# Phase A of a two-layer adaLN kernel: rows modulated on GpSimd instead of transposed back on TensorE

## The chip, the cores and the metric

The kernel runs on one core of a Trainium2 chip. A core has TensorE (PE) for matmuls, VectorE (DVE), ScalarE (ACT) and GpSimd (POOL) for the rest, and SyncE (SP), which issues most of the DMAs. The metric is the device time of one execution in microseconds; the median of some timed runs is given. A profile is one execution more, taken with the hardware profiler.

## What is computed

Two transformer layers act on x, of shape (4, 1024, 256), fp32 throughout. A row of x is a token; a batch is one of the four sequences. Each layer normalises x, scales and shifts it per batch (the modulation), runs an attention-like block, adds the result times a gate, and does the same again with a mixture of experts. Phase A is the first half of layer 0 and the modulation and routing of its second half. Cut to that:

```python
mod = (silu(L0_c) @ L0_wmod).reshape(4, 6, 1, -1)
sa, ca, ga, sb, cb, gb = (mod[:, i] for i in range(6))
ga, gb = (the sign of each) * maximum(abs(each), 0.25)
h = layernorm(x) * (1 + ca) + sa
x = x + ga * attn(h)            # bilinear attention, no softmax
h = layernorm(x) * (1 + cb) + sb
x = x + gb * experts(h)         # 8 experts, the best 2 of each token
```

The attention has no softmax, so for a batch it reduces to h times a 256 x 256 matrix (block-diagonal in the kernel's layout), made from h's Gram matrix, the queries, the combiners and the gate ga.

## The kernel before, in words

Phase A loads x, computes shifts, scales and gates, and then does for each batch a first half (`first_half`) and a second half (`second_half`). A batch has 8 chunks of 128 tokens, worked on in two groups (g = 0, 1) of four.

A group's rows are normalised by ACT (`normalised`, L968, four instructions of 128x256, into a buffer xn1 or xn2). PE transposes them to features on partitions (`to_features`, L1008, eight transposes). ACT takes them out of PSUM and modulates in the same instruction (L1013), since shift and scale are one number per partition there; this gives h1T or h2T. But the rows with tokens on partitions are needed too, modulated. So `to_tokens` transposes h1T or h2T back (L1035, eight transposes, named pm_b) and ACT copies the result out (L1040, two copies of 128x512) into h1 or h2.

In the first half the modulated rows h1 feed the Gram matrix (`gram`, L1102, 32 matmuls a batch, after all of the batch's rows are there). Its diagonal blocks are multiplied with the combiners (`head_t1`, L1134) and the queries (`head_m`, L1155) and then with the gate ga0 (`head_m_out`, L1167); the result is md. In the second half h1T times md gives the attention's output (L1195), DVE adds it to x (L1205), and the new rows are normalised, transposed and modulated again. h2T feeds the router's logits (L1235), DVE picks the experts (`route`), and the modulated rows h2 are stored to DRAM, to `h_rows` (L1270), from which the expert phase gathers its tokens.

Shifts and scales are made with features on partitions (`mods_by_feature`, L883 on PE, then DVE into modT). The gates ga and gb are made as rows of four partitions (`gate_row`, `gate_of`), and `gates` spreads each batch's rows over 128 partitions with matmuls against a selecting matrix `pick` (`spread`, L335, named pm_bc); ACT copies them into ga0 and gb0 (L927, L928).

The order on PE, ACT, DVE and POOL is not the program's but that of a planner (`Plan`): each piece of work has an engine, a supposed duration, pieces that it comes after, buffers that it holds and a rank (low first). The planner plays the pieces through in time, and their instructions are written in the order in which they begin. `FIRSTS` and `SECONDS` are the ranks of the batches' halves. SP's DMAs are pieces too, but SP is not among the engines whose order is fixed (`ORDERED`), in Phase A. Buffers are counted in `Plan(...)`: three of xn1, two of xn2, one h1, four h2.

Ahead of the plan SP loads x (L218), small tensors, and the first contents of the two expert weight buffers (L236, L237; 1028 KB and 1152 KB, twice). They hold the last expert, so that blocks of that expert need no gather; they are first read by the expert phase. ACT's queue loads the modulation weights of layer 0 (L204); those of layer 1 come later into the same buffer, from SP, and are multiplied near the end of Phase A (L1319). Phase A ends with a chain that makes the lists of the experts' blocks (turn, total, close, limits, L440 to L761), after which POOL fetches the first rows of `h_rows` (L348) and PE starts on the experts (L1610).

Of the kernel before, what the change touches and what calls it, by code (L numbers as in the profile page):

```python
# [8 lines left out]
F32 = mybir.dt.float32  # L9
F16 = mybir.dt.float16  # L10
I32 = mybir.dt.int32
AF = mybir.ActivationFunctionType
ALU = mybir.AluOpType
# [124 lines left out]
def adaln_d2_kernel(  # L138
# [92 lines left out]


    w1buf = [pw.tile([P, W1ROW], F32, name=f"w1_{i}") for i in range(2)]
    w2buf = [pw.tile([P, W2ROW], F32, name=f"w2_{i}") for i in range(2)]
    for i in range(2):
        nc.sync.dma_start(w1buf[i], W1[(E - 1) * P :, :])  # L236
        nc.sync.dma_start(w2buf[i], W2[(E - 1) * P :, :])  # L237

    xgbuf = [pw.tile([P, D], F32, name=f"xg_{i}") for i in range(4)]
# [7 lines left out]
    for e in range(E):  # L247
        nc.gpsimd.memset(rank[:, e : e + 1], float(E - e))

    pick = pa.tile([B, B, P], F32, name="pick", bufs=1)  # L250
    nc.gpsimd.memset(pick, 0.0)
    nc.gpsimd.affine_select(
        out=pick,
        in_=pick,
        compare_op=ALU.not_equal,
        fill=1.0,
        base=0,
        pattern=[[-1, B], [0, P]],
        channel_multiplier=1,
    )  # L260
    ones16 = const.tile([P, P], F16, name="ones16")
# [46 lines left out]
    def silu_of(layer, cT):  # L308
        sT = small.tile([P, KD, B], F32, name=f"sT{layer}")
        nc.scalar.activation(sT, cT, AF.Silu)  # L310
        return sT

    def mod_rows(sT, w, at, n):

        pr = psum(ps_2, [B, n], "pm_mod")
        for k in range(KD):
            nc.tensor.matmul(
                pr, lhsT=sT[:, k, :], rhs=w[:, k, at : at + n], start=(k == 0), stop=(k == KD - 1)
            )
        return pr  # L320

    def gate_of(dst, src, scratch):
# [7 lines left out]
        nc.vector.scalar_tensor_tensor(dst, sign, -1.0, size, ALU.add, ALU.mult)  # L330

    def spread(b, rows):

        pb = psum(ps_m, [P, rows.shape[1]], "pm_bc")
        nc.tensor.matmul(pb, lhsT=pick[:, b, :], rhs=rows, start=True, stop=True)  # L335
        return pb

# [500 lines left out]

    modT = const.tile([P, 4, KD, B], F32, name="modT")
    SA, CA, SB, CB = range(4)  # L840
# [16 lines left out]

    plan = Plan(p1=3, p2=2, pm=3, xn1=3, h1T=2, h1=1, xn2=2, h2T=2, h2=4, t1=1)
    PE, ACT, DVE, POOL = "PE", "ACT", "DVE", "POOL"
# [14 lines left out]
    def mods_by_feature(which, column, at):  # L874
        ps = plan.slot("p1")

        def mm():
            pf = tiles["modT", which] = psum(ps_1, [P, 2 * KD, B], "pm_modT")
            for i in range(2):
                for q in range(KD):  # L880
                    c = column[i] * D + q * P
                    for k in range(KD):
                        nc.tensor.matmul(  # L883
                            pf[:, i * KD + q, :],
                            lhsT=wm0[:, k, c : c + P],
                            rhs=sT0[:, k, :],
                            start=(k == 0),
                            stop=(k == KD - 1),
                        )

        def out_():
            pf = tiles["modT", which]
            nc.vector.tensor_copy(modT[:, which[0], :, :], pf[:, :KD, :])
            nc.vector.tensor_scalar(
                modT[:, which[1], :, :], pf[:, KD:, :], 1.0, None, ALU.add
            )

        i = plan(PE, 1.8, mm, holds=[ps], at=at, rank=-1)
        return plan(DVE, 0.4, out_, after=[i], holds=[ps], rank=-1)

    def gate_row(i, column, at):
# [13 lines left out]
        )  # L915

    def gates(after):
        done = []
        for b in range(B):
            ps = plan.slot("pm")  # L920

            def mm(b=b):
                tiles["spread", b] = spread(b, gate_rows.rearrange("b i d -> b (i d)"))

            def out_(b=b):
                pb = tiles["spread", b]
                nc.scalar.copy(ga0[:, b, :], pb[:, :D])  # L927
                nc.scalar.copy(gb0[:, b, :], pb[:, D:])  # L928

            m = plan(PE, 0.9, mm, after=after, holds=[ps], rank=b - 0.4)  # L930
            done.append(plan(ACT, 0.8, out_, after=[m], holds=[ps], rank=b - 0.4))
        return done

# [65 lines left out]
    def to_features(b, g, key, slot, dst, held, shift, scale, after, rank):  # L999

        done = []
        for k in range(KD):
            ps = plan.slot("pm")

            def mm(k=k):
                pt = tiles["pt", key, k] = psum(ps_m, [P, 4, P], "pm_t")
                for i in range(4):
                    nc.tensor.transpose(  # L1008
                        pt[:, i, :], tiles["xn", key][:, i, k * P : (k + 1) * P], ident
                    )  # L1010

            def out_(k=k):
                nc.scalar.activation(  # L1013
                    dst()[:, k, :, :],
                    tiles["pt", key, k],
                    AF.Identity,
                    bias=modT[:, shift, k, b : b + 1],
                    scale=modT[:, scale, k, b : b + 1],
                )

            m = plan(PE, 0.55, mm, after=after, holds=[ps, slot, held], rank=rank)
            done.append(plan(ACT, 0.67, out_, after=[m], holds=[ps, held], rank=rank))
        return done

    def to_tokens(key, src, held, dst, to, after, rank):

        done = []
        for i in range(2):
# [10 lines left out]
            def out_(i=i):  # L1039
                nc.scalar.copy(dst()[:, 2 * i : 2 * i + 2, :], tiles["pb", key, i])  # L1040

            m = plan(PE, 0.55, mm, after=after, holds=[ps, held, to], rank=rank)
            done.append(plan(ACT, 0.6, out_, after=[m], holds=[ps, to], rank=rank))
        return done
# [12 lines left out]

    FIRSTS, SECONDS, SPLIT = [0.0, 1.89, 1.82, 2.75], [1.66, 2.89, 3.45, 2.92], 2

    def first_half(b, arrival):  # L1060

        rank = FIRSTS[b]
        held, to = plan.slot("h1T"), plan.slot("h1")
        hT = buffer(("h1T", b), "h1T", [P, KD, NC, P])
        h = buffer(("h1", b), "h1", [P, NC, D])
        whole = []
        for g in range(2):
            key, slot = (1, b, g), plan.slot("xn1")
            n = normalised(
                b, range(4 * g, 4 * g + 4), key, slot, lambda c: [], rank, arrival[g]  # L1070
            )
            cs = slice(4 * g, 4 * g + 4)
            f = to_features(
                b,
# [9 lines left out]
            )  # L1084
            whole += to_tokens(
                key,
                lambda cs=cs: hT()[:, :, cs, :],
                held,
                lambda cs=cs: h()[:, cs, :],
                to,  # L1090
                f,
                rank,
            )

        ps, gd, md = plan.slot("p1"), gds[b % 2], mds[b % 2]

        def gram(j, cs):
            if j == 0 and cs[0] == 0:
                tiles["gram", b] = psum(ps_1, [P, KD, P], "pm_gram")
            for c in cs:  # L1100
                hj = h()[:, c, j * P : (j + 1) * P]
                nc.tensor.matmul(  # L1102
# [12 lines left out]
        for j in range(KD):  # L1115
            for cs in (range(4), range(4, NC)):
# [5 lines left out]
                        after=m,  # L1122
                        holds=[ps, to],
                        rank=rank,
# [38 lines left out]
        def head_m_out():  # L1163
# [12 lines left out]
            head_m_out,  # L1176
            after=[m, gates0[b], *before],
            holds=[ps],
# [4 lines left out]
    def second_half(b):  # L1183
# [34 lines left out]
        for g in range(2):  # L1218
# [4 lines left out]
            hT2, held2 = buffer(("h2T", b, g), "h2T", [P, KD, 4, P]), plan.slot("h2T")  # L1223
            f = to_features(b, g, key, slot, hT2, held2, SB, CB, [*n, mods_b], rank)
            if b == SPLIT and g:
# [18 lines left out]
            if b == SPLIT:  # L1244
                of_batch["routed"] = ready[g][0]
            h2, to = buffer(("h2", b, g), "h2", [P, 4, D]), plan.slot("h2")
            backs[g] = (to_tokens(key, hT2, held2, h2, to, f, rank + 0.1), to, h2)
        for gs in routed:
# [16 lines left out]
            for g in gs:  # L1265
                back, to, h2 = backs[g]

                def store(g=g, h2=h2):
                    at = 4 * g * B * P
# [3 lines left out]
                        )[b],  # L1273
                        h2(),
                    )

                plan("SP", 4.0, store, after=back, holds=[to], rank=rank)

# [3 lines left out]

    mods_a = mods_by_feature((SA, CA), (0, 1), 7.5)
    mods_b = mods_by_feature((SB, CB), (3, 4), 12.0)
    rows_done = [gate_row(0, 2, 10.0), gate_row(1, 5, 12.0)]
    gates0 = gates(rows_done)
    for b in range(B):
# [21 lines left out]

    loaded = plan("SP", 0.3, load_wm1, after=[mods_a, mods_b, *rows_done])  # L1310
    for piece in range(3):
        ps = plan.slot("p2")
        m = loaded
        for k in range(KD):

            def mm(piece=piece, k=k):
                if k == 0:
                    tiles["rows1", piece] = psum(ps_2, [B, 2 * D], "pm_mod")
                nc.tensor.matmul(  # L1319
                    tiles["rows1", piece],  # L1320
                    lhsT=sT1[:, k, :],
                    rhs=tiles["wm1"][:, k, 2 * D * piece : 2 * D * (piece + 1)],
# [1133 lines left out]
```

## Time and profile before

| what | value |
|---|---|
| timed runs, median of 3 | 1171.77 us (1170.53 to 1175.14) |
| the profiled execution's own time | 1148.51 us |
| its span | 1146.5 us |
| mean granted TensorE clock | 0.988 |
| busy: PE, DVE, ACT, POOL | 1101.7, 589.4, 428.2, 413.8 us |
| first expert matmul (L1610) starts at | 124.98 us |
| last row store to h_rows issued at | 110.9 us |
| way back to rows, L1035 and L1040 | 128 transposes, 32 copies |
| spreading, L335, L927 and L928 | 8 matmul passes, 8 copies |

In a row of the profile, "out<-in" are the names of what is written and read, then come the shapes, "xN" is the number of instructions, then busy time and mean duration, and after the second bar the idle time ahead of them with what ended it. PEld is the weight load of PE, which overlaps its matmuls. A time in brackets in the timeline is the idle time just ahead of a line.

### The profile page before, as it was taken

To read this page: it belongs to the slowest core of one execution; us is meant where nothing else is said; L and a number is where in the kernel's file an instruction comes from. 1 tells how busy PE (TensorE), PEld (TensorE's weight loads), DVE (VectorE), ACT (ScalarE), POOL (GpSimd) and SP (SyncE) were. 2 spreads that over 40 slices of the span, in tenths; PEclk is the share of its full clock that TensorE was granted. 3 is DMA by queue.
4 is the path that set the end of the run, shared out by engine and by line. 5 is a ranking of instruction groups with operands and counts; after the bars stand their busy time and mean duration, and the time that the engine had idled before them with its cause. 6 is when DMAs were issued, how large, how long until landed. Compare 5 with 4: busy or idle time off the path is not lost. (4 is left out here: it accounts for less than half of the span.)

```text
span 1146.5 us, 18577 instructions
## 1 busy us (share of the span) xinstructions
PE 1101.7 (96%) x6244; PEld 873.2 (76%) x6244; DVE 589.4 (51%) x2243; ACT 428.2 (37%) x1156; POOL 413.8 (36%) x479
## 2 busy tenths in 40 slices
PE   9999899999999999999998999999999999999894
PEld 5997799999999999999988565665666676646651
DVE  7686332322122222222237598877677535787567
ACT  5967233323333322333325333423325325333321
POOL 2000334433443343334355452420125232536535
PEclk8999999999999999999999999999999999999988
DMA  9303423656441514242162221200028564337944
GB/s 341 121 23 111 140 83 102 218 170 202 133 153 37 190 38 152 74 152 80 38 216 71 74 65 47 65 19 19 0 78 245 167 169 137 102 99 214 283 131 142
DMA packets 88388, 140.50 MB, mean 123 GB/s; under 512 B 24730, under 2 KB 63136, under 8 KB 83684
## 3 DMA queue, kind: packets, MB, share of 16 engines
q0 software_dynamic: 31680, 69.61, 20.0%
q1 hardware_dynamic: 55508, 68.10, 18.5%
q10 hardware_dynamic: 1104, 1.58, 0.4%
q8 instruction: 51, 0.84, 0.3%
q14 instruction: 45, 0.37, 0.1%
HBM read 222.48 MB, written 30.57 MB: 221 GB/s over the span
## 5 line engine op out<-in xcount | busy, mean ns | idle before, releaser
L1622 ACT ACTIVATE hid<-p_h,w 128x128 f32<-128x128 f32 x544 | 154.9, 368 | 324.6 <-issue 263.7
L1610 PEld LDWEIGHTS p_h<-xT,w 128*128 128x128 f32 x2176 | 252.9, 192 | 7.8 <-DVE xT L1595 3.9
L1610 PE MATMUL p_h<-xT,w 128*128 128x128 f32 x2176 | 254.5, 275 | 4.0 <-DVE xT L1595 4.0
L1633 PE MATMUL p_y<-w,hid 128*128 128x256 f32 x1088 | 248.9, 382 | 0.0
L1890 PE MATMUL p_u<-hT,a 128*128 128x512 f32 x512 | 230.3, 596 | 2.4 <-ACT hf L1902 1.5
L348 POOL DMA_INDIRECT w<-in_W,g_wrow x134 | 133.8, 999 | 263.9 <-ACT hid L1622 121.4
L1633 PEld LDWEIGHTS p_y<-w,hid 128*128 128x128 f32 x1088 | 201.6, 190 | 24.6
L1890 PEld LDWEIGHTS p_u<-hT,a 128*128 128x128 f32 x512 | 93.8, 190 | 101.3 <-issue 89.9
L1595 DVE COPY xT<-pm_x 128x256 f32<-128x256 f32 x68 | 28.8, 424 | 177.0 <-PE pm_x L1590 176.8
L1644 DVE TENSOR_TENSOR y<-p_y,w 128x256 f32<-128x256 f32 x68 | 28.8, 424 | 172.1 <-PE p_y L1633 172.1
L1938 PE MATMUL p_f<-a,hf 128*128 128x256 f32 x512 | 115.3, 380 | 0.0
L348 POOL DMA_INDIRECT xg<-h_rows,g_row x68 | 65.7, 966 | 129.6 <-DVE g_hits L752 109.1
L1938 PEld LDWEIGHTS p_f<-a,hf 128*128 128x128 f32 x512 | 96.3, 190 | 15.5 <-issue 2.9
L348 POOL DMA_INDIRECT yg<-y,g_slot x64 | 61.5, 961 | 83.6 <-DVE x_sb L1467 45.2
L2203 PE MATMUL p_e<-we,xT 128*128 128x256 f32 x280 | 73.2, 393 | 4.1 <-DMA we<-in_ew 3.5
L1902 ACT ACTIVATE hf<-p_u,decay 128x512 f32<-128x512 f32 x56 | 38.1, 683 | 67.6 <-PE p_u L1890 65.1
L2203 PEld LDWEIGHTS p_e<-we,xT 128*128 128x128 f32 x280 | 50.1, 194 | 14.7 <-issue 5.5
L1986 POOL TENSOR_TENSOR x_sb<-x_sb,step 128x256 f32<-128x256 f32 x32 | 24.2, 758 | 99.3 <-DVE step L1979 87.5
L348 POOL DMA_INDIRECT xg<-ga_rows,ga_row x39 | 37.1, 950 | 53.2 <-DVE g_hits L752 19.4
L1530 DVE TENSOR_TENSOR h<-h,mod 128x256 f32<-128x256 f32 x128 | 50.9, 422 | 5.8 <-ACT h L1520 3.4
L1906 DVE SCALAR_TENSOR_TENSOR hf<-p_u,decay,hf 128x512 f32<-128x512 f32 x56 | 41.9, 748 | 17.2 <-PE p_u L1890 13.5
L2213 ACT COPY y<-p_e 128x256 f32<-128x256 f32 x70 | 25.8, 371 | 60.1 <-PE p_e L2203 27.2
(368 smaller groups left out, 1295.7 us busy)
## 6 DMA issues: line engine op xcount, KB each, us to landing
we<-in_ew SPq DMA_DIRECT2D x70, 256.0 KB, 3.8
y<-y SPq DMA_DIRECT2D x68, 128.0 KB, 1.8
ga_y<-y SPq DMA_DIRECT2D x39, 128.0 KB, 3.3
x_sb<-in_x SPq DMA_DIRECT2D x8, 512.0 KB
h_rows<-h SPq DMA_DIRECT2D x8, 512.0 KB, 3.6
gb_y<-y SPq DMA_DIRECT2D x31, 128.0 KB, 4.7
out_x<-x_sb SPq DMA_DIRECT2D x7, 512.0 KB, 3.1
a<-in_fw SPq DMA_DIRECT2D x6, 512.0 KB
```

The source lines that it names most:

```text
L348: return nc.gpsimd.indirect_dma_start(out=dst, out_offset=None, in_=table, in_offset=bass.IndirectOffsetOnAxis(ap=index, axis=0), bounds_c ...
L1530: nc.vector.tensor_tensor(h, h, mods1[(sc, sh)[i]][:, b, :], (ALU.mult, ALU.add)[i])
L1595: nc.vector.tensor_copy(xT, pt)
L1610: nc.tensor.matmul(p1[:, i, :], lhsT=w1[:, k * H + m * P : k * H + (m + 1) * P], rhs=xT[:, k, :], start=(k == 0), stop=(k == KD - 1),)
L1622: nc.scalar.activation(hid[:, m, :], p1[:, i, :], AF.Relu, bias=w1buf[j % 2][:, KD * H + m : KD * H + m + 1],)
L1633: nc.tensor.matmul(p2, lhsT=hid[:, m, :], rhs=w2[:, m * D : (m + 1) * D], start=(m == 0), stop=(m == KH - 1),)
L1644: nc.vector.tensor_tensor(y, p2, w2buf[j % 2][:, KH * D :], ALU.add)
L1890: nc.tensor.matmul(pu, lhsT=a[:, k, m * P : (m + 1) * P], rhs=made["n1", c, "hT"][:, k, :, :], start=(k == 0), stop=(k == KD - 1),)
L1902: nc.scalar.activation(made[key, m], made[key, m, 0], AF.Silu, scale=decays[c])
L1906: nc.vector.scalar_tensor_tensor(h, made[key, m, 1], decays[c], h, ALU.mult, ALU.mult)
L1938: nc.tensor.matmul(made[key, "p2", b], lhsT=made[key, m][:, b * P : (b + 1) * P], rhs=a1[:, m, :], start=(m == 0), stop=(m == KH - 1),)
L2203: nc.tensor.matmul(made[key, "p2"], lhsT=made[key, "xT"][:, k, :], rhs=made[key, "we"][:, k * D : (k + 1) * D], start=(k == 0), stop=(k == ...
```

## The change

Half of the groups no longer get their rows by the way back. For batch 1 in the first half, and for the groups (batch, g) = (0,0), (0,1), (1,0), (1,1), (2,0), (3,0) in the second, POOL modulates the normalised rows in place, with two multiplications and two additions of 128 x (2 x 256) each per group (`modulated`). It starts when PE has read the rows for their transposes. The other groups keep the transposes, and these now write over the normalised rows; h1 and h2 are gone, and xn1 and xn2 have four buffers each.

POOL needs shifts and scales as rows on all partitions (`spread0`). So modT, now ordered batch before feature half, is transposed by PE (one transpose for each pair), copied out by ACT, stored to DRAM by SP, and loaded back by SP with a partition broadcast (1 MB a pair). The gates go the same way: gate_rows to DRAM, then one broadcast load each into ga0 and gb0. `pick`, `spread` and `gates` go. The first loads of the expert weights move into the plan, after the broadcast loads, and layer 1's modulation weights come after them. The silu of c is padded with zeros from 4 to 64 columns for the matmuls of `mods_by_feature`. The ranks of the halves are others.

The diff, cut to its core:

```diff
-    for i in range(2):
-        nc.sync.dma_start(w1buf[i], W1[(E - 1) * P :, :])
-        nc.sync.dma_start(w2buf[i], W2[(E - 1) * P :, :])
...
-        sT = small.tile([P, KD, B], F32, name=f"sT{layer}")
-        nc.scalar.activation(sT, cT, AF.Silu)
+        sT = pa.tile([P, KD, ROUTER], F32, name=f"sT{layer}", bufs=1)
+        nc.vector.memset(sT, 0.0)
+        nc.scalar.activation(sT[:, :, :B], cT, AF.Silu)
...
-    plan = Plan(p1=3, p2=2, pm=3, xn1=3, h1T=2, h1=1, xn2=2, h2T=2, h2=4, t1=1)
+    plan = Plan(p1=3, p2=2, pm=3, xn1=4, h1T=2, xn2=4, h2T=2, t1=1)
...
+        def turn():
+            pr = tiles["rows0_ps", which] = psum(ps_m, [2 * B * KD, P], "pm_rows")
+            nc.tensor.transpose(
+                pr, modT[:, pair, :, :].rearrange("p w b k -> p (w b k)"), ident
+            )
...
+        def store():
+            nc.sync.dma_start(
+                mod_rows0[pair, :, :].rearrange("w b (k p) -> (w b k) p", p=P),
+                tiles["rows0", which],
+            )
+
+        def load():
+            nc.sync.dma_start(spread0[:, pair, :, :], mod_rows0[pair, :, :].partition_broadcast(P))
+
+        m = plan(PE, 0.12, turn, after=[d], holds=[ps], rank=-0.9)
+        a = plan(ACT, 0.25, turned, after=[m], holds=[ps], rank=-0.9)
+        q = plan("SP", 0.1, store, after=[a], rank=-0.9, lag=2.2)
+        return d, plan("SP", 0.1, load, after=[q], rank=-0.9, lag=4.5)
...
+    def modulated(b, key, slot, shift, scale, after, rank):
+
+        done = []
+        for i in range(2):
+            last = after
+            for of, op in ((scale, ALU.mult), (shift, ALU.add)):
+
+                def do(i=i, of=of, op=op):
+                    h = tiles["xn", key][:, 2 * i : 2 * i + 2, :]
+                    nc.gpsimd.tensor_tensor(
+                        h, h, spread0[:, of, b, :].unsqueeze(1).to_broadcast([P, 2, D]), op
+                    )
+
+                last = [plan(POOL, 1.45, do, after=last, holds=[slot], rank=rank)]
+            done += last
+        return done
...
-    FIRSTS, SECONDS, SPLIT = [0.0, 1.89, 1.82, 2.75], [1.66, 2.89, 3.45, 2.92], 2
+    FIRSTS, SECONDS, SPLIT = [0.0, 1.66, 1.65, 3.35], [1.8, 3.42, 3.5, 2.62], 2
+
+
+    POOL1, POOL2 = (1,), ((0, 0), (0, 1), (1, 0), (1, 1), (2, 0), (3, 0))
...
+            if b in POOL1:
+                whole += modulated(b, key, slot, SA, CA, [*turned, spread_a], rank)
+            else:
+                whole += to_tokens(key, slot, lambda cs=cs: hT()[:, :, cs, :], held, f, rank)
...
-            after=[m, gates0[b], *before],
+            after=[m, gate_loaded, *before],
...
-    gates0 = gates(rows_done)
+
+    def gates_out():
+        nc.sync.dma_start(gates0, gate_rows)
+
+    def gate_in(i, dst):
+        nc.sync.dma_start(dst, gates0[:, i, :].partition_broadcast(P))
+
+    q = plan("SP", 0.1, gates_out, after=rows_done, rank=-0.8, lag=2.2)
+    gate_loaded = plan("SP", 0.1, lambda: gate_in(0, ga0), after=[q], rank=-0.8, lag=3.5)
+
+    def first_weights():
+
+        for i in range(2):
+            nc.sync.dma_start(w1buf[i], W1[(E - 1) * P :, :])
+            nc.sync.dma_start(w2buf[i], W2[(E - 1) * P :, :])
+        gate_in(1, gb0)
+
+    weights0 = plan("SP", 0.5, first_weights, after=[spread_a, spread_b, gate_loaded])
...
-    loaded = plan("SP", 0.3, load_wm1, after=[mods_a, mods_b, *rows_done])
+    loaded = plan("SP", 0.3, load_wm1, after=[weights0])
```

## Prediction

> **What bounds the kernel now.** I first read the busy shares in 40 slices. TensorE (PE) is at 9 tenths nearly everywhere, while the granted clock and the DMA share show that the first slices are different: the queues are full and PE is not. The change touches only Phase A, which ends where the first expert matmul starts, so I cut that stretch out with the table of stages.
>
> ```profile
> core 0: us, PE busy (x) PEld busy (x) DVE busy (x) ACT busy (x) POOL busy (x), PEclk, DMA share, GB/s
> ...
> 23.00:26.00 3.00, 2.90 (x8) 1.43 (x9) 2.66 (x15) 1.36 (x5) 0.00 (x0) 0.56 1.03 422
> 26.00:29.00 3.00, 3.00 (x16) 3.00 (x16) 1.89 (x10) 2.71 (x7) 0.00 (x0) 0.50 1.00 416
> ...
> 32.00:109.00 77.00, 73.86 (x651) 68.40 (x650) 55.51 (x225) 60.48 (x118) 0.00 (x0) 1.00 0.21 71
> ```
>
> From 32 to 109 us PE runs 73.9 of 77 us, at full clock, with the DMA engines mostly idle and GpSimd (POOL) not used at all. ScalarE (ACT) is second with 60.5 us. So this stretch is a PE stream with some ACT waits. Before 32 us it is a chain of hand-offs behind the loads, at half clock for part of it. Next the groups of instructions of that stretch, PE's and then ACT's:
>
> ```profile
> L1035 PE MATMUL pm_b<-ident,h2T 128*128 128x128 f32 x56 | 8.2, 277 | 1.1 <-ACT h2T L1013 1.1
> L1035 PE MATMUL pm_b<-ident,h1T 128*128 128x128 f32 x48 | 7.1, 277 | 0.0
> ```
>
> ```profile
> L1040 ACT COPY h<-pm_b 128x512 f32<-128x512 f32 x26 | 14.1, 592 | 1.9 <-PE pm_b L1035 1.9
> ```
>
> These are the transposes back to rows, 8 pairs of weight load and matmul to a group of four chunks, and the two copies of 592 ns that follow. A matmul's 277 ns overlaps the next one, so its price is the spacing of starts, which the timeline gives. The timeline also has the start, the gate and the end:
>
> ```profile
> 23.10 1.83 PE L335 MATMUL pm_bc<-gate_rows,pick 4*128 4x512 f32 x2 [0.43 <-ACT h1T L1013]
> ```
>
> ```profile
> 36.08 0.59 DVE L1167 TENSOR_TENSOR md<-pm_m,ga 64x128 f32<-64x128 f32 x2
> ...
> 36.82 3.19 PE L1195 MATMUL pm_o<-md,h1T 128*128 128x128 f32 x24 [0.35 <-DVE md L1167]
> ```
>
> ```profile
> 88.16 0.92 PEld L1035 LDWEIGHTS pm_b<-ident,h2T 128*128 128x128 f32 x8
> ...
> 89.05 1.86 PEld L1235 LDWEIGHTS pm_l<-wr_sb,h2T 128*128 128x128 f32 x16
> ```
>
> ```profile
> 120.80 1.12 POOL L348 DMA_INDIRECT xg<-h_rows,g_row  x1 [109.15 <-DVE g_hits L752]
> ...
> 124.98 3.81 PE L1610 MATMUL p_h<-xT,w 128*128 128x128 f32 x32 [0.56 <-DVE xT L1595]
> ```
>
> Eight weight loads of the way back start at 88.16 and the next kind at 89.05: 0.89 us for 8, so 111 ns a pair. The last router matmul ends at 109.1; from there routing, list and first fetch are one serial chain to 120.8, and the experts start at 125.0. From there on PE is busy to the end. So I take it that a microsecond taken out before 109 moves everything after it by a microsecond.
>
> **What the Trainium skill says.** "TensorE: Matmul & The Clock Gate", LDWEIGHTS: the load time is the number of columns over 1.2, 107 ns for 128. The 111 ns agree: the stream is paced by weight loads. "GPSIMD Engine Reference", 3.1: a two-input fp32 add of 2048 elements takes 4497 ns. The trace has it smaller, and in another stage:
>
> ```profile
> L1986 POOL TENSOR_TENSOR x_sb<-x_sb,step x32: 721/732/899, 668.9 to 1081.8; 128x256 f32<-128x256 f32 x32
> ```
>
> A line through both (732 at 256, 4497 at 2048) has a slope of 2.10 ns, so 1.27 us at 512 elements, an estimate; twice 732, or 1.46 us, is the upper bound without contention. The same page, Key points: POOL shares its SBUF interfaces with VectorE (DVE), against its instructions with two SBUF inputs or in a two-port mode. DVE's large items here are statistics with one input and an addition with one input in PSUM, so I expect little; no run yet shows POOL beside them. "DMA: Bandwidth & Descriptors", Two DMAs through the same engine are not ordered: a load that reads what an earlier DMA stored must wait for its completion. So each row that goes through DRAM costs SP a full round trip.
>
> **The change part by part.**
>
> *Transposes back* go for batch 1's first half (2 groups) and for six of eight groups of the second halves. 8 groups x 8 pairs x 0.111 = **7.1 us** off PE, all in the stretch in which it is the bound. ACT loses 16 x 0.592 = 9.5 us. Where the tail follows ACT instead of PE (93 to 107 us, a cycle of four normalisations 2.06, two h2T 1.45 and two copies 1.05), dropping the copies gives 1.05 a group, so the value holds there as well. Bounds 5 (two of the eight groups already hidden in ACT waits) to 8.
>
> *Spreading matmuls and their copies* go: 8 passes, 4.9 us busy, and 8 copies of about 0.38. All passes and 6 of the copies lie before 26 us, where the chain of batch 0 decides. The way back of its second group starts at 24.87 behind the pass at 23.10, although its input is ready at about 23.8: 1.0 us. ACT's four copies between 18.98 and 21.62 stand before normalisations of the same group, up to 1.4 us. Part is lost again, since fewer matmuls may leave the clock at 0.5 to 0.56 for as long. I take **1.5 us** (0 to 2.4).
>
> *Added on PE and ACT*: two transposes of 16 rows (0.11 each), two small copies (0.25, as the cast of 128x128), 64 instead of 4 moving columns in 32 pairs: the router's pairs with 64 run at 1.92/16 = 120 ns, the present ones at 1.84/16 = 115, so 0.2 us. Together 0.3 to 0.9, half in waits that exist: **0.4 us**. Two clears of DVE and the changed order of the eight columns cost nothing, hidden behind the loads of x that DVE waits 4.3 us for.
>
> *POOL* gets 8 x 4 = 32 operations x 1.27 to 1.46 = 41 to 47 us in some 75 us in which it is idle. A group takes 4 x 1.27 = 5.1 to 5.8 us in place of 0.9 on PE and 1.2 on ACT, so latency, not rate, is the price. Batch 1's Gram matmuls wait for both groups; behind them on PE, whose order is fixed, stands everything planned later. Batch 2's first half is ranked beside it and fills PE meanwhile. In the second halves only the store waits for POOL. The last queue is (1,0), (1,1), (2,0): if their rows are ready from about 84 us, three groups end at 84 + 3 x 5.8 = 101.4; stored with a landing of 3.6 us, that is 105. The fetch will stand near 120.8 - 6.7 = 114, so there are 9 us in hand. The buffers hold longer too (normalised rows until the store is read), with 4 instead of 2 or 3 of them. I charge **1.5 us** for hand-offs (0 to 5).
>
> *SP* gets two stores and two 1 MB loads of the spread rows, one store and two 0.5 MB loads of the gates; 4.4 MB of first weights, then wmod1, come behind them instead of in front. At the 400 GB/s of 20 to 32 us a MB takes 2.6 us. x is in by some 19 us (6 MB of x, wmod and small ones at 370 GB/s from 2 us), the store of shifts and scales behind it lands at 20, its load at 25, the second pair at 28, ga0 at about 31. The first md needs ga0 at 36.1 - 1.5 = 34.6: 3.5 us in hand, so nothing charged; without that cover each further MB in front costs 2.6 us. The first weights are read at 125 us and the wmod1 rows at 110, so their delay is hidden by 70 us.
>
> Sum: -7.1 - 1.5 + 0.4 + 1.5 = **-6.7 us**. The profiled execution has a span of 1146.5 and a time of 1148.5, and would go to 1141.8. The timed runs have a median of 1171.8, 23 us above it; I carry the microseconds over: **1165.1**.
>
> **Rivals.** *The rows come late (slower).* SP's order isn't that of the code:
>
> ```profile
> 27.98 7.11 SPq L1393 DMA_DIRECT2D y<-ones  x6
> ...
> 55.14 56.08 SPq L1270 DMA_DIRECT2D h_rows<-h  x8
> ```
>
> Line 1393 comes after the whole plan, and yet goes ahead of its stores: what is ready is pulled forward. The first weights depend on nothing. If they and wmod1 slip ahead of the loads, the queues are full to 35 us, as now; two spread loads, ga0 and a round trip of 3.6 us then give 35 + 2.6 + 2.6 + 1.3 + 3.6 = 45. PE stops at the first md for 45 - 34.6 = 10.5 us: -6.7 + 10.5 = +4, about **1176** (to 1180 with batch 1 late as well). It decides from a landing of 41 us on. Against it: wmod1, which depends on Phase A's first matmuls, went ahead of the ready ones now, so the order isn't purely what is ready first; then one or two weights slip in, 3 to 6 us.
>
> *POOL's latency takes the place of the transposes (no change).* If batch 1's Gram stands 4 to 6 us on PE, because its rows or its 10 to 12 us of POOL come late, or the granted clock drops in that hole, the net is 1 to 3 us: **1170**.
>
> *The clean case.* Hand-offs cost nothing and the start gains its 2.4: 8 + 2.4 - 0.4 = 10: **1162**.
>
> **How the numbers follow.** Forecast around 1165 (own range 1162 to 1169): 0.50. Clean, 1162 and below: 0.13. No change, 1169 to 1174: 0.22. Late rows, 1174 to 1180: 0.15. About 0.5%, 5.9 us, is what a measurement of this kernel can tell from no change, so faster means below 1165.9: 0.66 of the forecast and all of clean, 0.33 + 0.13 = 0.46. Slower means above 1177.6: 0.11, the upper part of the late case. The rest, 0.43, is the same. The range 1160 to 1176 leaves out the upper half of the late case and a few hundredths below.
>
> **What would show it.** Right: the first expert matmul near 118 instead of 125 us; 64 fewer pairs of L1035; POOL operations of 1.27 to 1.46 us; the first md at about 34.5 with no wait on a DMA; the last row store at least 3 us before the fetch. Wrong: a wait of md on ga0, or of POOL on the spread rows; Gram waiting for POOL; POOL above 2 us an operation, when the last store comes near the fetch (12 operations x 0.7 eat the 9 us); DVE's statistics above 411 ns, which would be the shared interface; or a later stage that takes the gain back.

## The result and the profile after

| what | before | after |
|---|---|---|
| timed runs on one chip, median of 11 each | 1170.53 us | 1179.74 us |
| ratio, 95% interval | | 1.0067 [1.0048, 1.0087] |
| the profiled execution: time, span, clock | 1170.55, 1168.5 us, 0.980 | 1177.0, 1175.3 us, 0.973 |
| last router matmul ends at | 110.21 us | 119.18 us |
| first expert matmul starts at | 126.12 us | 136.73 us |
| from there to the end of the span | 1042.4 us | 1038.6 us |

The change makes the kernel slower, by 0.67% or 7.8 us. (The two medians are 9.2 us apart; here and below a difference in us is the ratio, which draws on all runs, times the time before.) The forecast was 1165.1 us, and 1179.7 lies above its range.

Chips differ: the kernel before takes 1152 us on some and 1172 on others, and the profile in the first part of this document, of an execution of 1148.5 us, fits one of the quicker ones. The column "before" of the four lower rows is therefore the trace of a repeat of the kernel before (experiment 8), on a chip where its median is 1172.0. The loss, 10.6 us in these two traces, arises before the first expert matmul, and 9.0 of it before the last router matmul. So I read that stretch first, from 32 us on, in the table of stages: the repeat of before, then after.

```profile
core 0: us, PE busy (x) PEld busy (x) DVE busy (x) ACT busy (x) POOL busy (x), PEclk, DMA share, GB/s
32.00:110.21 78.21, 75.12 (x663) 69.67 (x662) 56.36 (x229) 62.08 (x123) 0.00 (x0) 1.00 0.20 70
```

```profile
32.00:119.18 87.18, 74.70 (x569) 70.09 (x568) 76.48 (x217) 50.72 (x96) 40.12 (x32) 0.86 0.28 101
```

PE has 94 matmuls fewer (64 are the transposes that went; most of the others ran ahead of 32 us, 149 against 126) and is just as long busy: its clock is 0.86 where it was 1.00. It is idle for 12.5 us where it was idle for 3.1. And DVE, with 12 instructions fewer, is busy for 20.1 us more. That is the line to follow. DVE's groups in this part of Phase A, first the repeat of before from 32 to 110 us (a row that stays the same and one that doesn't), then after from 30 to 121 us, so that both have eleven groups of rows:

```profile
L942 DVE BATCH_NORM_STATS2 ln_st<-x_sb 128x6 f32<-128x256 f32 x40 | 16.4, 410 | 0.3
...
L961 DVE SCALAR_TENSOR_TENSOR ln_m<-ln_mv,ln_y 128x4 f32<-128x4 f32 x11 | 1.8, 162 | 0.4
```

```profile
L940 DVE BATCH_NORM_STATS2 ln_st<-x_sb 128x6 f32<-128x256 f32 x40 | 16.4, 411 | 0.3
...
L959 DVE SCALAR_TENSOR_TENSOR ln_m<-ln_mv,ln_y 128x4 f32<-128x4 f32 x11 | 8.7, 789 | 0.4
...
L955 DVE SCALAR_TENSOR_TENSOR ln_t<-ln_y 128x4 f32<-128x4 f32 x11 | 6.1, 557 | 0.4
L956 DVE TENSOR_TENSOR ln_t<-ln_t,ln_v 128x4 f32<-128x4 f32 x11 | 5.9, 537 | 0.4
...
L957 DVE SCALAR_TENSOR_TENSOR ln_y<-ln_t,ln_y 128x4 f32<-128x4 f32 x11 | 4.7, 424 | 0.4
```

The statistics, the largest item, take 411 ns as before. Four instructions on 128x4 numbers each, the Newton step of the reciprocal root and the shift that the normalisation adds, had 162 or 163 ns each and now have 424 to 789 in the mean. Together they take 25.4 us in place of 7.2, so some 18 of DVE's 20.1 us. How one such mean comes about is seen in the timeline: DVE, then POOL and PE at the same place (start, duration; in brackets the idle time ahead).

```profile
45.11 1.04 DVE L955 SCALAR_TENSOR_TENSOR ln_t<-ln_y 128x4 f32<-128x4 f32 x1
46.18 0.16 DVE L956 TENSOR_TENSOR ln_t<-ln_t,ln_v 128x4 f32<-128x4 f32 x1
46.38 1.12 DVE L957 SCALAR_TENSOR_TENSOR ln_y<-ln_t,ln_y 128x4 f32<-128x4 f32 x1
47.53 1.19 DVE L959 SCALAR_TENSOR_TENSOR ln_m<-ln_mv,ln_y 128x4 f32<-128x4 f32 x1
48.64 0.58 DVE L1181 TENSOR_TENSOR md<-pm_m,ga 64x128 f32<-64x128 f32 x2
```

```profile
44.85 20.64 POOL L1054 TENSOR_TENSOR xn<-xn,spread 128x512 f32<-128x512 f32 x16 [33.30 <-ACT t L1158]
```

```profile
49.28 1.16 PE L1209 MATMUL pm_o<-md,h1T 128*128 128x128 f32 x8 [2.23 <-DVE md L1181]
```

From 44.85 us POOL runs 16 instructions without a gap. Each is 1.27 us long, and a DVE instruction beside it takes 0.16 us or something just below 1.27, as if it stood until the POOL instruction ended. Behind three such instructions stands md, which is not longer itself (two in 0.58 us, 288 ns each before): it only comes late. PE, whose order is fixed, stands 2.23 us for it. PE's waits from 32 to 121.5 us (total, times, longest):

```profile
PE pm_o L1209 <- DVE md L1181: 4.3, 3, 2.2
PE pm_l L1249 <- ACT h2T L1011: 3.9, 5, 2.1
PE pm_t L1148 <- DVE gd L1126: 2.8, 2, 2.5
```

These three are 11.0 of PE's idle time; in the repeat of before the same three waits are 1.0. The first is md queued behind such steps on DVE. The third is gd (the copy of the Gram matrix out of PSUM): in its longest wait it stands in DVE's order behind a routing that itself starts only when the last stretched steps are over, at 65.5 us. The second is one link further. ACT's order is fixed too, and ahead of h2T stands a normalisation that waits for ln_m, the last step of the chain:

```profile
52.68 0.60 ACT L966 ACTIVATE xn<-x_sb,ln_m,ln_y 128x256 f32<-128x256 f32 x1 [1.27 <-DVE ln_m L959]
```

The rest of the loss is the clock. The same thirty weight loads of the router, at two places of the trace of after:

```profile
98.31 3.42 PEld L1249 LDWEIGHTS pm_l<-wr_sb,h2T 128*128 128x128 f32 x30 [0.40 <-ACT h2T L1011]
...
107.53 6.47 PEld L1249 LDWEIGHTS pm_l<-wr_sb,h2T 128*128 128x128 f32 x30 [0.73 <-ACT h2T L1011]
```

114 ns a load, then 216. In steps of half a us the clock of this trace is 1.00 from 32 us on, except for four stretches at 0.50: about 54.5 to 61, 71.5 to 74.5, 92 to 95 and 105.5 to 115.5 us. So the balance of the stretch from 32 us is, against the repeat of before: 94 pairs fewer at 0.111 give -10.4; PE's busy time is nonetheless only 0.4 lower, and I put the difference, +10.0, down to the lower clock (74.70 us at 0.86 instead of 1.00 would be 10.5, which agrees); PE's idle time is +9.4. Sum +9.0, which is 87.18 - 78.21.

What the prediction looked for otherwise: the transposes back that remain (count, then shortest, median and longest in ns), POOL's own instructions, the first md, and the end of the phase.

```profile
L1034 PE MATMUL pm_b<-ident,h1T x48: 272/273/476, 18.1 to 78.0; 128*128 128x128 f32 x48
...
L1034 PE MATMUL pm_b<-ident,h2T x16: 272/273/421, 114.0 to 119.8; 128*128 128x128 f32 x16
```

```profile
L1054 POOL TENSOR_TENSOR xn<-xn,spread x32: 1257/1267/1329, 44.9 to 114.1; 128x512 f32<-128x512 f32 x32
```

```profile
33.54 0.59 DVE L1181 TENSOR_TENSOR md<-pm_m,ga 64x128 f32<-64x128 f32 x2
```

```profile
132.14 1.15 POOL L330 DMA_INDIRECT xg<-h_rows,g_row  x1 [16.69 <-DVE g_hits L734]
...
136.73 3.48 PE L1644 MATMUL p_h<-xT,w 128*128 128x128 f32 x29 [0.56 <-issue]
```

The first md comes at 33.54 us (36.08 in the first trace of before, 37.24 in the repeat), without a wait on ga0. POOL ends its last row at 115.4, 16.7 us ahead of the first fetch, so the row stores hold nothing up.

### The profile page after: what moved, and what is told of

It is laid out like the page before. It is cut to its first block, busy times and chain, and to the rows that moved or that the text cites. A ratio compares the mean times of both kernels' runs of the same rounds, so it can differ in the third digit from the quotient of the medians.

```text
span 1175.3 us, 18478 instructions
## 1 busy us (share of the span) xinstructions
PE 1107.3 (94%) x6174; PEld 879.3 (75%) x6174; DVE 612.8 (52%) x2245; ACT 419.0 (36%) x1134; POOL 453.1 (39%) x509
## 5 line engine op out<-in xcount | busy, mean ns | idle before, releaser
L1644 PE MATMUL p_h<-xT,w 128*128 128x128 f32 x2176 | 257.8, 277 | 6.6 <-DVE xT L1629 3.7
L1644 PEld LDWEIGHTS p_h<-xT,w 128*128 128x128 f32 x2176 | 256.2, 194 | 10.4 <-DVE xT L1629 4.0
L1972 PE MATMUL p_f<-a,hf 128*128 128x256 f32 x512 | 115.5, 380 | 0.4 <-DVE step L2013 0.4
L2237 PEld LDWEIGHTS p_e<-we,xT 128*128 128x128 f32 x280 | 50.8, 197 | 19.7 <-issue 11.8
L1054 POOL TENSOR_TENSOR xn<-xn,spread 128x512 f32<-128x512 f32 x32 | 40.1, 1270 | 63.8 <-ACT t L1158 53.2
```

The lines of the kernel that those rows point to most:

```text
L1054: nc.gpsimd.tensor_tensor(h, h, spread0[:, of, b, :].unsqueeze(1).to_broadcast([P, 2, D]), op)
L1644: nc.tensor.matmul(p1[:, i, :], lhsT=w1[:, k * H + m * P : k * H + (m + 1) * P], rhs=xT[:, k, :], start=(k == 0), stop=(k == KD - 1),)
L1972: nc.tensor.matmul(made[key, "p2", b], lhsT=made[key, m][:, b * P : (b + 1) * P], rhs=a1[:, m, :], start=(m == 0), stop=(m == KH - 1),)
L2237: nc.tensor.matmul(made[key, "p2"], lhsT=made[key, "xT"][:, k, :], rhs=made[key, "we"][:, k * D : (k + 1) * D], start=(k == 0), stop=(k == ...
```

## The experiments

**My theory** after the traces: while a POOL instruction on SBUF tensors runs, a DVE instruction that needs the interface shared with POOL (two SBUF inputs) stands until it ends. The price of a short DVE step is then set by the length of POOL's instruction and not by its own, and such steps stand in the normalising chain ahead of ACT and PE. **Rivals,** with the numbers that the expectations use: (1) the rows and gates through DRAM, the buffers and the new order of the halves; (2) POOL's latency, since a group's rows take 5.1 us and others may wait for them.

Ratios are against the kernel before on the same chip. Experiments 1 to 4 ran on one chip (before 1152.2 us), 5 to 8 on another (1172.0), 9 to 11 on a third (1153.0), 12 on a fourth (1172.05). The changed kernel itself was timed only in the comparison above, so a difference of two ratios is in most cases one between chips.

### 1. The kernel before, with POOL busy beside it

Nothing of the change is in this kernel. POOL gets 32 multiplications of 128x512 on a scratch tile of its own, planned where the change has its groups.

```diff
+    BESIDE = ((1, 1, 0), (1, 1, 1), (2, 0, 0), (2, 0, 1), (2, 1, 0), (2, 1, 1), (2, 2, 0), (2, 3, 0))
...
+        for _ in range(4):
...
+                nc.gpsimd.tensor_tensor(idle, idle, idle_by.unsqueeze(1).to_broadcast([P, 2, D]), ALU.mult)
+            after = [plan(POOL, 1.45, do, after=after, rank=rank)]
...
+        if key in BESIDE:
+            beside([m], rank)
```

> The kernel before with 32 multiplications of 128x512 on POOL beside it, on a scratch tile of its own, planned behind the same eight groups' transposes as in the changed kernel; nobody waits for them. Theory (POOL and DVE share an SBUF interface, and a DVE instruction with two SBUF inputs waits until the running POOL instruction is over, 0.16 us becoming 1.1): 6 to 12 us slower than before, Newton steps of over 1 us beside POOL. Rival 1 (the rows and gates through DRAM, the buffers and the new order of the halves cost the time) and rival 2 (PE waits for POOL's results, Gram first): within 2 us of before, Newton steps as before.

Measured: 1160.75 us, ratio 1.0068 [1.0048, 1.0089], +7.8 us. POOL's instructions wait for nobody, so they ran in one piece at the start; DVE's third Newton instruction beside them:

```profile
12.49 43.21 POOL L1009 TENSOR_TENSOR idle<-idle,idle_by 128x512 f32<-128x512 f32 x32
```

```profile
L963 DVE SCALAR_TENSOR_TENSOR ln_y<-ln_t,ln_y x16: 161/163/1125, 10.0 to 107.6; 128x4 f32<-128x4 f32 x16
```

POOL work that nobody reads, waits for or stores costs as much as the whole change loses. Latency, DMAs and order are excluded as its cause here.

### 2. The change without POOL

```diff
-    POOL1, POOL2 = (1,), ((0, 0), (0, 1), (1, 0), (1, 1), (2, 0), (3, 0))
+    POOL1, POOL2 = (), ()
```

All groups go the way back over PE; gates by DMA, buffers and ranks stay those of the change.

> The changed kernel with no group on POOL: all rows come back by the transposes, everything else of the change stays (gates and rows through DRAM, four buffers each, new ranks). Theory: the loss of 9 us is gone, 0 to 3 us below or above before. Rival 1: still 7 to 10 us slower than before. Rival 2: as the theory, since POOL has no work.

Measured: 1146.66 us, ratio 0.9951 [0.993, 0.9972], -5.6 us.

```profile
L957 DVE SCALAR_TENSOR_TENSOR ln_y<-ln_t,ln_y x16: 161/161/165, 11.1 to 98.8; 128x4 f32<-128x4 f32 x16
```

The longest of the sixteen is 165 ns now. So it is the POOL part of the change that loses, about 7.8 + 5.6 = 13.4 us, although it takes 64 pairs off PE; all else in the change gains, more than the 0 to 3 us expected. Where it gains is not clear: in the single traces only 0.8 us of it stand before the first expert matmul (124.21 us, and 124.98 in the first trace of before).

### 3. and 4. The normalising chain without two-input instructions, after and before

In the chain I left out the Newton step (the root of ACT is used as it is) and made the shift with instructions of one tensor input, their other operands being pointers to scalars. Experiment 3 has this edit on the kernel after, experiment 4 on the kernel before, as the control.

```diff
-            nc.vector.scalar_tensor_tensor(t, y, -0.5, y, ALU.mult, ALU.mult)
-            nc.vector.tensor_tensor(t, t, v, ALU.mult)
-            nc.vector.scalar_tensor_tensor(y, t, 1.5, y, ALU.add, ALU.mult)
-            nc.vector.scalar_tensor_tensor(m, mv[:, :, 0], -1.0, y, ALU.mult, ALU.mult)
+            for i in range(n):
+                nc.vector.tensor_scalar(m[:, i:i+1], mv[:, i, 0:1], y[:, i:i+1], -1.0, ALU.mult, ALU.mult)
```

> The changed kernel with a normalisation that has no DVE instruction with two SBUF tensor inputs: the Newton step on the reciprocal root is left out (three instructions), and the product of mean and root is made with four instructions of one tensor input and a scalar from SBUF each. Theory: at least 6 of the 9 us come back, so 2 us slower than before to 5 us faster, and these instructions stay below 0.3 us beside POOL. Rival 1 and rival 2: still 6 to 9 us slower than before, as the chain is only some 0.2 us a group shorter.

> The control of the last one: the same normalisation, Newton step left out, in the kernel before. Every theory: 0 to 2 us faster than before, because PE sets the pace there and the DVE chain is hidden.

Measured: experiment 3 1154.79 us, 1.002 [1.0006, 1.0034], +2.3; experiment 4 1149.79, 0.9983 [0.9968, 0.9998], -2.0. The edit gains 2.0 us without POOL and 7.8 - 2.3 = 5.5 with it, a little less than the 6 expected, and it doesn't bring the time below that of before. The trace of experiment 3 shows why. First the new one-input instruction and the one that adds epsilon to the variance, over the whole of Phase A, then a group of the routing, two lines of the timeline beside POOL, and a wait of PE:

```profile
L956 DVE TENSOR_SCALAR ln_m<-ln_mv,ln_y x64: 201/204/216, 10.1 to 105.1; 128x1 f32<-128x1 f32 x64
...
L944 DVE TENSOR_SCALAR ln_v<-ln_mv x16: 169/170/1122, 7.4 to 95.1; 128x4 f32<-128x4 f32 x16
```

```profile
L399 DVE TENSOR_TENSOR r_hit<-r_hit,rank 128x64 f32<-128x64 f32 x6 | 4.5, 749 | 0.2
```

```profile
58.85 1.31 DVE L409 SCALAR_TENSOR_TENSOR r_rest<-g_one,r_l 128x64 f32<-128x64 f16 x1
60.20 0.22 DVE L393 TENSOR_REDUCE g_best<-r_rest 128x8 f32<-128x64 f32 x1
```

```profile
PE pm_t L1147 <- DVE gd L1125: 6.0, 2, 5.8
```

The new one-input instruction is never longer than 216 ns. But the routing of the earlier batches, which stands on the same DVE queue, is made of two-input instructions as well; they are still stretched, and gd behind them holds PE for up to 5.8 us. The reduction next to them, with one input, takes 0.22 us. So the cure of one place leaves the next one: the kind of instruction decides, not the part of the kernel it belongs to. One line doesn't fit my theory as I put it: ln_v has one tensor input, and takes up to 1.12 us in place of 0.17. Two SBUF inputs are therefore not the only kind that is held; ln_v may be an instruction in the "two-port mode" that the prediction names beside them, but no run shows the mode it ran in.

### 5. The same work of POOL in instructions half as long

```diff
-        for i in range(2):
+        for i in range(4):
...
-                    h = tiles["xn", key][:, 2 * i : 2 * i + 2, :]
-                    nc.gpsimd.tensor_tensor(h, h, spread0[:, of, b, :].unsqueeze(1).to_broadcast([P, 2, D]), op)
+                    h = tiles["xn", key][:, i, :]
+                    nc.gpsimd.tensor_tensor(h, h, spread0[:, of, b, :], op)
...
-                last = [plan(POOL, 1.45, do, after=last, holds=[slot], rank=rank)]
+                last = [plan(POOL, 0.725, do, after=last, holds=[slot], rank=rank)]
```

> The changed kernel with each POOL instruction cut in two: 64 of 128x256 in place of 32 of 128x512. Theory (a DVE instruction with two SBUF inputs waits for the end of the running POOL instruction): the longest Newton steps fall from 1.1 to 1.2 us to about 0.6 to 0.7, and although POOL works longer in all (64 x 0.73 = 47 us against 40), 3 to 5 us of the loss come back. Rival 2 (PE waits for POOL's results): POOL is slower by 7 us in all, so 0 to 3 us slower than the changed kernel.

Measured: 1174.9 us, 1.0031 [1.001, 1.0052], +3.6 us.

```profile
L1054 POOL TENSOR_TENSOR xn<-xn,spread 128x256 f32<-128x256 f32 x64 | 45.4, 728 | 54.7 <-ACT t L1156 48.8 <-ACT h2T L1011 2.3 <-PE pm_t L1006 1.2
```

```profile
L957 DVE SCALAR_TENSOR_TENSOR ln_y<-ln_t,ln_y x16: 161/162/649, 10.9 to 104.4; 128x4 f32<-128x4 f32 x16
```

POOL is busy for longer (45.4 in place of 40.1 us), a group takes longer, and yet 4.2 us come back. The longest DVE steps of the four are 649 to 741 ns. The stall follows the length of POOL's single instruction.

### 6. The kernel before, with one-input POOL instructions beside it

Against experiment 1:

```diff
-                nc.gpsimd.tensor_tensor(idle, idle, idle_by.unsqueeze(1).to_broadcast([P, 2, D]), ALU.mult)
+                nc.gpsimd.tensor_scalar(idle, idle, 0.5, 0.0, ALU.mult, ALU.add)
```

> As the kernel before with idle POOL work beside it, but the 32 POOL instructions of 128x512 have one input tensor and two immediates. Theory in its strict form (what collides is POOL's second input, or any POOL read): open between two forms. If only two-input POOL instructions hold DVE up, within 1 us of before and Newton steps at 0.16; if any POOL tensor instruction does, steps as long as the POOL instruction and a loss in proportion to its length. Rivals 1 and 2: within 2 us of before.

Measured: 1175.12 us, 1.0027 [1.0017, 1.0038], +3.2 us.

```profile
13.01 22.52 POOL L1009 TENSOR_SCALAR idle<-idle 128x512 f32<-128x512 f32 x32
```

```profile
L963 DVE SCALAR_TENSOR_TENSOR ln_y<-ln_t,ln_y x16: 161/164/474, 10.6 to 100.5; 128x4 f32<-128x4 f32 x16
```

POOL doesn't need two inputs for it. An instruction of 0.62 us holds these four steps for up to 615 ns, one of 1.27 us for up to 1.13 us; the loss goes with it, 3.2 to 7.8 us.

### 7. The change, POOL's instructions half as long by having one input

POOL multiplies by 1 and adds 0 in the same place, the same number of times. The modulation of these rows is left out.

```diff
-                    nc.gpsimd.tensor_tensor(h, h, spread0[:, of, b, :].unsqueeze(1).to_broadcast([P, 2, D]), op)
+                    nc.gpsimd.tensor_scalar(h, h, 1.0, 0.0, ALU.mult, ALU.add)
```

> The changed kernel in which POOL's 32 instructions multiply by one and add zero, with one input tensor: the modulation of these rows is left out, all waits on POOL's results stay. Theory, if one-input POOL instructions leave DVE alone: the loss is gone, 5 to 8 us faster than before. Rival 2 (waiting for POOL): most of the loss stays if the instructions last as long as now, and falls with their length if they are shorter. Rival 1: the loss stays.

Measured: 1159.88 us, 0.9897 [0.9879, 0.9916], -12.1 us. The stage from 32 us to the last router matmul:

```profile
32.00:102.77 70.77, 66.51 (x587) 61.77 (x586) 61.64 (x230) 52.16 (x100) 19.43 (x32) 1.00 0.36 132
```

DVE is busy for 61.6 us and not 76.5, PE is idle for 4.3 and not 12.5, and its clock is 1.00. This comes near to what the prediction had in mind as its clean case: the pairs off PE and little loss at the hand-offs. It is more than the 5 to 8 us expected, and for another reason, since experiment 6 shows that one-input POOL instructions don't leave DVE alone. POOL's work is half of what the change needs, so both the stalls and the latency are shorter here; in experiment 12 the latency is put back.

### 8. The kernel before again

> The kernel before, unchanged, for a trace on the same chip as the others. All theories: same time as before within 0.3%, Phase A's last router matmul at about 109 us.

Measured: 1172.0 us, 1.0003 [0.9991, 1.0015]. A ratio that is more than some 1.5 thousandths off 1 is thus not the comparison's own. Its trace is the one used above.

### 9. Without POOL and with the ranks of before

Experiment 2 with one more line changed back:

```diff
-    FIRSTS, SECONDS, SPLIT = [0.0, 1.66, 1.65, 3.35], [1.8, 3.42, 3.5, 2.62], 2
+    FIRSTS, SECONDS, SPLIT = [0.0, 1.89, 1.82, 2.75], [1.66, 2.89, 3.45, 2.92], 2
```

> The changed kernel with no group on POOL and the ranks of the halves from the kernel before. It tells what of the gain of the version without POOL (5.6 us) comes from the gates and the buffers and what from the ranks. If from the gates and buffers: 4 to 7 us faster than before. If from the ranks: within 2 us of before.

Measured: 1150.54 us, 0.9977 [0.9959, 0.9996], -2.7 us, where experiment 2 has -5.6. It is neither of what I expected but halfway between: some 3 us of that gain belong to the ranks, some 3 to gates, loads and buffers. The two intervals just overlap, so I don't part it more finely.

### 10. and 11. Is there a version that is faster? One-input chain without POOL, and with short POOL instructions

Experiment 10 is experiment 2 with the edit of experiment 3; experiment 11 is experiment 5 with it.

> The changed kernel with no group on POOL and the normalisation without the Newton step (left out, as in the two runs before with it). With no POOL work there is nothing for DVE to wait for, so it should gain only what it gained in the kernel before, 2 us: 6 to 9 us faster than before.

> The changed kernel with POOL's instructions cut in two and the normalisation without the Newton step (left out). If both act on the same stall, by making it shorter and rarer: 1 us slower to 3 us faster than before, better than either alone (+3.6 and +2.3 us).

Measured: experiment 10 1144.49 us, 0.9929 [0.9903, 0.9954], -8.2; experiment 11 1145.92, 0.9939 [0.9914, 0.9964], -7.0. Experiment 11 was expected between 1 us slower and 3 us faster: a miss in size. The two cures together do more than I had added up, from +7.8 for the change to -7.0; yet with POOL at work and 64 pairs fewer on PE it still isn't ahead of experiment 10, where POOL does nothing. From the last router matmul to the first expert matmul it takes 20.0 us, where the repeat of before has 15.9 and experiment 10 has 16.6. Part of this is the same stall: the routing that ends this chain has two-input instructions too, and POOL still runs beside it until 102.05 us (at 97.84 us a step that has 0.19 us alone takes 0.43, at 100.65 another takes 0.65).

### 12. As 7, with the number of POOL instructions doubled

64 one-input instructions; a group takes 5.0 us as in the change, and POOL is busy as long. The modulation is left out as in 7. Against experiment 7:

```diff
-                    nc.gpsimd.tensor_scalar(h, h, 1.0, 0.0, ALU.mult, ALU.add)
+                    for _ in range(2):
+                        nc.gpsimd.tensor_scalar(h, h, 1.0, 0.0, ALU.mult, ALU.add)
```

> As the run in which POOL multiplies its rows by one with one input tensor, but each instruction twice: 64 instructions of 0.62 us, so that a group takes POOL 5.0 us, as in the changed kernel (5.1). The modulation of these rows is left out; all waits on POOL's results stay, and as long as in the changed kernel. Theory (the stalls of DVE cost the time, and end with the running POOL instruction): as long in POOL but stalls of at most 0.6 in place of 1.2 us, so well below the changed kernel: 6 us faster to 3 us slower than before. Rival 2 (PE and the buffers wait for POOL's results): the loss comes back, 6 to 10 us slower than before.

Measured: 1167.06 us, 0.9966 [0.9951, 0.9982], -4.0 us.

```profile
L1055 POOL TENSOR_SCALAR xn<-xn 128x512 f32<-128x512 f32 x64 | 39.4, 623 | 54.6 <-ACT t L1157 47.3 <-ACT h2T L1011 3.4
```

```profile
32.00:105.65 73.65, 66.88 (x575) 61.56 (x574) 63.84 (x216) 50.96 (x98) 39.36 (x64) 0.98 0.30 111
```

Same order, same DMAs, same pairs off PE, same latency of a group, same 40 us of POOL as the change, only in pieces of 0.62 instead of 1.27 us, with one input instead of two: 4.0 + 7.8 = 11.8 us better. POOL's latency therefore is not what made the change slow. How much of the 11.8 is the length of the piece and how much the second input isn't parted: experiment 5, with two inputs and pieces of 0.73 us, stays at +3.6, and in its trace one wait of PE on gd, 5.2 us long, makes much of that (the longest here is 2.9). Against experiment 7 it costs 8.1 us to have twice as many; how much of that is latency and how much are further stalls isn't parted.

## Why the prediction was wrong, point by point

**The step that failed** is the sentence "DVE's large items here are statistics with one input and an addition with one input in PSUM, so I expect little", by which contention had no term in the sum. About the items that it names it is right: statistics 410 to 411 ns, additions with one input in PSUM 675 before and 677 after. But it weighed DVE's instructions by their busy time. What an instruction pays for waiting is set by the other engine's instruction, and so it must be weighed by count and place: 44 short two-input instructions in the groups above, some 162 ns each, in the chain that feeds ACT and PE. With some 18 us more of them on DVE, PE was idle for 9.4 us more and lost about 10.0 to a lower clock, where the sum had nothing.

The page of the Trainium skill that the sentence leaned on does name these instructions. Another of its pages, "SBUF — State Buffer", Who interferes with whom, says more, and the prediction did not draw on it: "only the shared port pair causes contention, and it's an exclusive lock"; a DVE instruction with two SBUF inputs contends with a GpSimd instruction that reads SBUF, and the later one stands until the first has ended. The runs agree: longest steps of 1.20 us beside POOL's 1.27 us, 0.74 beside 0.73, 0.62 beside 0.62, and no stretch of a reduction (0.22 us), of the instruction with scalar pointers (216 ns at most), or where one input is in PSUM. With that, contention could have had a term. POOL is busy for 40.1 of the 87.2 us, so of 44 instructions some 20 meet it; at half to all of 1.27 us each that is 13 to 26 us of DVE time, an estimate from these traces, and some 18 were measured. What such time on DVE costs PE doesn't follow from it.

**"Latency, not rate, is the price"** was wrong as well: neither was. The 1.5 us charged for hand-offs stood where a stall should have stood. The trace names no wait of PE for POOL. Three waits of ACT ahead of a normalisation, 10.8 us in all, end with a POOL instruction, and the timeline puts two of them down to it. One of these, and the DVE step that ended with it:

```profile
90.63 2.08 ACT L966 ACTIVATE xn<-x_sb,ln_m,ln_y 128x256 f32<-128x256 f32 x4 [2.41 <-POOL xn L1054]
```

```profile
89.44 1.11 DVE L959 SCALAR_TENSOR_TENSOR ln_m<-ln_mv,ln_y 128x4 f32<-128x4 f32 x1
```

In all three ACT starts 0.08 us after the end of a stretched ln_m, which it needs. As a stretched step ends with POOL's instruction, the releaser that the profile infers can't tell the two apart, and these waits are no evidence of a wait for buffers.

**The transposes back.** Right: 64 pairs went (48 with h1T and 16 with h2T remain), and they count: experiment 7, where little stalls, has the stretch 7.4 us shorter than the repeat of before (78.21 to 70.77), part of it the earlier start.

**The start.** Right in direction, and too small: the first md came at 33.54 us (34.5 forecast), which is 2.5 us ahead of the first trace of before and 3.7 ahead of the repeat, above the upper bound of 2.4. The prediction feared that fewer matmuls might leave the clock low; it was higher, 0.91 in the mean from 14 to 32 us, where the traces of before have 0.74 and 0.64. The rows' loads were not late; the slower rival, late rows, didn't occur. One first weight load did slip ahead, at 18.57 us, without effect.

**POOL's instruction.** Right: 1.27 us, as the line through two durations gave. The last row was ready long before the fetch.

**What would make it wrong.** I had named "DVE's statistics above 411 ns" as the sign of the shared interface. It looked at the wrong instruction: the statistics are just those that can't show it.

**Foreseen only within a rival:** the clock. The prediction let it drop in a hole of PE in its case of no change, and gave it nothing in its sum. That the holes lower it is argued from this: in the stretch from 32 us to the last router matmul, PE idle for 12.5, 11.6 and 10.3 us goes with a mean clock of 0.86, 0.92 and 0.90 (the change, experiments 3 and 5), and idle for 6.8, 4.4 and 4.3 us with 0.98, 0.96 and 1.00 (experiments 12, 9 and 7). The size of a single hole doesn't decide it: the one of 2.23 us ahead of 49.28 us isn't followed by a slower clock, and the longest slow stretch follows five waits of 0.2 to 0.6 us each, between 102.7 and 105.6. Clock and holes were not varied apart.

**Left open.** The first expert matmul moves in single traces 0.6 to 6.3 us less favourably than the timed medians (after: +10.6 against +7.8; experiment 7: -6.8 against -12.1). How the loss divides between normalising and routing is known only roughly: experiment 3 takes 5.5 us away, of which 2.0 are its own gain in experiment 4. Routing without two-input instructions was not tried.

## What to carry to other kernels

Before work is given to POOL, list the DVE instructions that will run beside it by number of SBUF inputs and by place in the chain, not by busy time, and charge each two-input one up to the length of one POOL instruction. An instruction with one input isn't safe for that alone, as ln_v shows; look for it in a trace with POOL at work. Where they can't be rewritten, cut POOL's work into short instructions: halving them brought back 4.2 us although POOL worked longer. An engine that is idle in the profile isn't free as long as it shares a way to memory with one that isn't.

## What the runs showed of the hardware that I had not expected

- Beside POOL, a two-input DVE instruction of 0.16 us takes up to 1.20 us (POOL instruction 1.27 us), up to 0.74 (0.73) or up to 0.62 (0.62). POOL's own instructions hardly vary (1257 to 1329 ns).
- A one-input POOL instruction of 128x512 takes 0.62 us and holds DVE up as well. A 128x4 tensor_scalar of DVE with both tensors in SBUF (ln_v, 0.17 us) is held too, up to 1.04 us in the kernel after; the 128x1 form with scalar pointers is not.
- 12.5 us of idle PE in 87 us, in holes of at most 2.5 us, came with a mean clock of 0.86: four stretches at 0.50, the longest some 10 us, in which a weight load of 114 ns took 216.
